# A decoder layer with a mixture of experts: slots given group by group, and the experts' work divided into two bursts and a dense last group

## The chip, the cores and the metric

The kernel runs on one core of one Trainium2 chip. The metric is the device time of one execution in microseconds (us). Before the change the median of 9 runs is 855.45 us, the lowest 849.18, the highest 859.21. The profiled execution took 858.79 us; its span from the first to the last instruction is 857.0 us.

The core has five engines with queues of their own, each working through its instructions in order: PE (TensorE, matrix products), DVE (VectorE), ACT (ScalarE, which also issues DMAs), POOL (GpSimd, which also issues the indirect DMAs) and SP (which here only issues DMAs). They wait for one another by semaphores. SBUF is the on-chip memory of 128 partitions, PSUM holds PE's results, and DRAM holds inputs, outputs and scratch.

## The reference

x and enc are (32, 128, 128): 32 batch rows of 128 tokens with 128 features. One decoder layer in f32, with 16 heads of 8 features:

```
x  = layernorm(x + attn(x, x, x, causal))           # self-attention
x  = layernorm(x + attn(x, enc, enc))               # cross-attention
w  = softmax(x @ router_w + router_b)               # 8 experts
top2 values of w -> softmax -> combine weights of the token's two experts
h  = gelu(x @ e_w1[e] + e_b1[e])                     # 128 -> 512
eo = h @ e_w2[e] + e_b2[e]                           # 512 -> 128
x  = layernorm(x + sum over the token's two experts of combine * eo)
```

The reference computes every expert for every token and weights six of the eight by zero.

## The kernel before

Tokens are handled in groups of G = 4 batch rows; there are 8 groups of self-attention (s0 to s7) and 8 of cross-attention (c0 to c7).

**Attention.** A unit is one batch row of one kind, and there are 64. The list `order` (L607) sets their order: 11 units of s, then c and s in turn, then the 11 units of c that are left, so that LEAD = 11 rows of self-attention run ahead. Each unit takes two half slots (L690 to L705). In half slot h = 2t + half, `both_scores` computes half the heads' scores of unit t, whose row maxima DVE takes (L389), and half the transposed scores of unit t-2, with the maxima subtracted by a matrix product (L366), whose exponentials ACT takes (L397). For s units POOL then zeroes what the causal mask excludes (L401). `split` on POOL cuts the maxima into three bf16 parts, `maxima` turns them, `values` multiplies by V (L431), and `outputs` turns and divides by the sums.

**Work of a group.** A dictionary `table` names what else is traced after which half slot (L634 to L663): fetching the rows, turning them, keys, queries, values, then `project` with the residual and the normalization, `hand_over` from s to c, `keep_x2`, and `route` in five steps. `normalize` (L237) takes mean and variance on DVE and the root on POOL; the last scaling, four instructions (L249), is on the engine passed in: POOL in the attention, DVE at the end. Since tracing order is each engine's order, a step in `table` queues behind what stands before it on that engine.

**Slots.** Each token goes to two experts. The tokens are put into slots, 128 to a block, and a block belongs to one expert. PHASES = ((0, 24), (24, 8)) makes two phases, of 24 and 8 batch rows. `place(p)` (L534) runs once a phase, after its last group was routed: counts by expert, blocks wanted beyond the first of each expert, their starts, every token's rank, and a table of which block has which expert. The first 8 blocks of a phase are fixed, one to an expert; ND more are given as needed, 47 and 15, so the phases have NBL = 55 and 23 blocks. Then `scatter` (L583) sends each batch row twice by indirect DMA on POOL to its slots in DRAM (`xs`), 64 in all, each after a small memset.

**Experts.** After all attention, a loop goes through the 78 blocks (L826). All experts' weights are packed in SBUF (`wpk`: w1, w2, b1, b2 of an expert side by side, 4624 bytes a partition). A fixed block reads its expert's weights in place; for a given block SP loads the expert's number from the table, and a DMA copies the weights from `wpk` to one of five buffers `wd` (L743), four blocks ahead. Rows come four blocks at a time (`fetch_rows`, three buffers), PE turns them, `first_layer` runs 4 matrix products and 4 Gelu on ACT, `second_layer` runs 4 more and DVE adds b2 (L782). Finished blocks go to DRAM (`eo`).

**Gathering.** When a phase's blocks are done, `gather` (L791) fetches each token's two results by indirect DMA on POOL, 64 in all, and `combine` (L802) weights them, adds x2, normalizes and writes out. x2 of all tokens stays in SBUF.

**Loads.** All weights and constants are issued from ACT's queue (L157 to L196), and so is the clearing of `xs` with zeros (L232), 3520 and 1472 KB; the first x is fetched from SP.

Of the kernel before, what the change touches and what calls it, by code (L numbers as in the profile page):

```python
# [17 lines left out]
P = 128  # L18
# [6 lines left out]
PHASES = ((0, 24), (24, 8))  # L25
NP = len(PHASES)
NS = E

ND = [(2 * n * 128 - E) // 128 for _, n in PHASES]
NBL = [NS + n for n in ND]  # L30
XB = 4
W2 = FF
B1 = W2 + FF
B2 = B1 + NFC
WP = B2 + P
VC = 32
RG = 4
NPART = 3
LEAD = 11
EPS = 1e-05  # L40
# [14 lines left out]
def kernel(  # L55
# [39 lines left out]
    keep = ctx.enter_context(tc.tile_pool(name="keep", bufs=1))  # L95
# [4 lines left out]
    ident16 = const.tile([P, P], BF16, name="ident16")  # L100
    nc.vector.tensor_copy(ident16, ident)

# [13 lines left out]

    hm4 = const.tile([P, RG, 4], F32, name="hm4")
# [10 lines left out]
    nc.vector.tensor_reduce(hmask, hm4.rearrange("p g r -> p r g"), AX.X, ALU.add)  # L128


    mp4 = const.tile([P, RG, NPART, 4], F32, name="mp4")
# [5 lines left out]
    mpart = const.tile([P, 4], F32, name="mpart")  # L137
# [9 lines left out]

    apart = const.tile([1, 1], F32, name="apart")
    mhalf = const.tile([P, G], F32, name="mhalf")
    nc.gpsimd.memset(mhalf, -0.5)  # L150
    iota_i = const.tile([P, E], mybir.dt.int32, name="iota_i")
    nc.gpsimd.iota(iota_i, pattern=[[1, E]], base=0, channel_multiplier=0)
    iota_e = const.tile([P, E], F32, name="iota_e")
    nc.vector.tensor_copy(iota_e, iota_i)


    def load(src, shape, name):  # L157
        t = const.tile(shape, F32, name=name)
        nc.scalar.dma_start(out=t, in_=src)
        return t  # L160

    def column(src, name):
        return load(src.rearrange("(p o) -> p o", o=1), [P, 1], name)

    def row(src, n, name):
        return load(src.rearrange("(o n) -> o n", o=1).broadcast_to([P, n]), [P, n], name)

    class Attn:
        def __init__(self, wq, bq, wk, bk, wv, bv, wo, bo, n):
            self.wk = load(wk, [P, P], f"wk{n}")  # L170
            self.bk = column(bk, f"bk{n}")
            self.wq = load(wq, [P, P], f"wq{n}")
            self.bq = column(bq, f"bq{n}")
            self.wv = load(wv, [P, P], f"wv{n}")
            self.bv = column(bv, f"bv{n}")
            self.wo = load(wo, [P, P], f"wo{n}")
            self.bo = row(bo, P, f"bo{n}")

            self.bqm = const.tile([P, 4], F32, name=f"bqm{n}")
            nc.vector.tensor_scalar(self.bqm, hmask, self.bq, None, ALU.mult)  # L180

    sa = Attn(sa_wq, sa_bq, sa_wk, sa_bk, sa_wv, sa_bv, sa_wo, sa_bo, "s")
    ca = Attn(ca_wq, ca_bq, ca_wk, ca_bk, ca_wv, ca_bv, ca_wo, ca_bo, "c")
# [6 lines left out]
    b1 = load(e_b1.rearrange("e (c f) -> (e c) f", f=P), [E * NFC, P], "b1")  # L190


    wpk = const.tile([P, E, WP], F32, name="wpk")
    nc.scalar.dma_start(
        out=wpk[:, :, B2:], in_=e_b2.unsqueeze(0).broadcast_to([P, E, P])
    )  # L196


    def counted(shape, pattern, base, name):
        i = const.tile(shape, I32, name=f"{name}_i")  # L200
        nc.gpsimd.iota(i, pattern=pattern, base=base, channel_multiplier=0)
        f = const.tile(shape, F32, name=name)
        nc.vector.tensor_copy(f, i)
        return f

# [3 lines left out]
        fill=0.0, base=0, channel_multiplier=-1,  # L209
    )  # L210
    NF = max(n for _, n in PHASES) - 1
    full = counted([P, E, NF], [[0, E], [P, NF]], P, "full")
    e_col = counted([P, E, E], [[1, E], [0, E]], 0, "e_col")
    e_row = counted([P, E, E], [[0, E], [1, E]], 0, "e_row")
    lower = const.tile([P, E, E], F32, name="lower")
# [682 lines left out]
```

## Time and profile before

| What | us |
|---|---|
| Profiled execution, its own time | 858.79 |
| Its span, first to last instruction | 857.0 |
| Median of 9 runs | 855.45 |
| Busy in the span: PE | 579.5 |
| PE's weight loads, beside PE | 484.0 |
| DVE | 361.2 |
| ACT | 354.6 |
| POOL | 393.0 |

The mean clock granted to TensorE was 0.867 of full speed. DMA queues moved 73.87 MB, 86 GB/s in the mean.

A busy time is a share of the whole span, and the stages have different limits: read it by stretch. In the chain of work that ended last, "another core or an unknown queue" stands for a wait on something that the profile doesn't name as an instruction; here there is one core. Idle time of an engine costs nothing where another sets the pace.

### The profile page before, as it was taken

The numbers are of one execution on the slowest core, as the hardware profiler recorded it, in microseconds if no ns is written. First come the engines' busy times: TensorE is split into PE (matmuls) and PEld (weight loads), VectorE is DVE, ScalarE is ACT, GpSimd is POOL, SyncE is SP. The second block draws the span as 40 slices with busy tenths as digits, with TensorE's granted clock in tenths as the row PEclk, the third lists the DMA queues.
The fourth block names the chain that finished last, engine by engine and source line by source line (L and its number), as shares of the span: only waits on it lengthen the run. The fifth ranks groups of instructions, "written<-read, shape, count | busy, mean of one in ns | idle before, by whom it ended". The sixth has DMA issues, their size and how long they took to land.

```text
span 857.0 us, 21066 instructions
## 1 busy us (share of the span) xinstructions
PE 579.5 (68%) x8767; PEld 484.0 (56%) x8819; DVE 361.2 (42%) x996; ACT 354.6 (41%) x666; POOL 393.0 (46%) x698
## 2 busy tenths in 40 slices
PE   1488988889989899899989820009999980645200
PEld 0256666667667676677768610009999980645200
DVE  3035555556656566565667540002222210353426
ACT  0225656565666656665665300005555540223100
POOL 5025566536656366563544588870000027155271
PEclk9969999999999999999999755558999995778655
DMA  6800202002010000000000011124999945255121
GB/s 143 244 1 3 76 8 69 16 2 64 15 39 15 2 15 2 14 3 15 3 2 3 9 36 52 52 71 168 335 355 370 342 139 174 91 172 180 51 59 37
DMA packets 66911, 73.87 MB, mean 86 GB/s; under 512 B 6368, under 2 KB 55808, under 8 KB 66816
## 3 DMA queue, kind: packets, MB, share of 16 engines
q1 hardware_dynamic: 43360, 55.32, 18.6%
q10 hardware_dynamic: 19360, 8.81, 3.8%
q0 software_dynamic: 4096, 8.40, 3.3%
q8 instruction: 69, 1.13, 0.6%
q14 instruction: 26, 0.21, 0.1%
HBM read 19.30 MB, written 16.52 MB: 42 GB/s over the span
## 4 chain that ended last, share of the span: by engine, by line
PE 46%; another core or an unknown queue 11%; POOL 11%; DVE 10%; ACT 8%; DMA 5%; issue 5%; SPq 2%; ACTq 2%; POOLq 0%; DVEq 0%
PE po L778 7%; PE ph L761 6%; PE st_c L374 4%; PE st_s L374 4%; PE po_s L431 4%; DMA wd<-wpk 3%; ACT qb_c L327 3%; POOL pr_s L401 2%; PE po_c L431 2%; ACT qb_s L327 2%; POOL gt L797 2%; PE st_c L366 2%; POOL y_c L249 2%; PE st_s L366 2%
## 5 line engine op out<-in xcount | busy, mean ns | idle before, releaser
L797 POOL DMA_INDIRECT gt<-eo,slots x64 | 63.0, 984 | 151.3 <-ACT h L766 124.4
L389 DVE TENSOR_REDUCE m_s<-sc_s 128x8 f32<-128x1024 f32 x64 | 78.2, 1222 | 123.0 <-PE st_s L374 90.2
L401 POOL TENSOR_SCALAR_AFFINE_SELECT pr_s<-pr_s 128x1024 f32<-128x1024 f32 x64 | 69.9, 1096 | 90.2 <-ACT pr_s L397 90.2
L389 DVE TENSOR_REDUCE m_c<-sc_c 128x8 f32<-128x1024 f32 x64 | 78.1, 1220 | 68.4 <-PE st_c L374 48.8
L766 ACT ACTIVATE h<-ph,wd 128x128 f32<-128x128 f32 x248 | 70.6, 370 | 87.3 <-issue 26.8
L397 ACT ACTIVATE pr_s<-st_s 128x1024 f32<-128x1024 f32 x64 | 65.7, 1026 | 74.4 <-PE st_s L374 74.4
L778 PE MATMUL po<-wd,h 128*128 128x128 f32 x496 | 70.7, 289 | 25.4 <-ACT h L766 21.1
L397 ACT ACTIVATE pr_c<-st_c 128x1024 f32<-128x1024 f32 x64 | 65.6, 1025 | 52.6 <-PE st_c L374 51.9
L778 PEld LDWEIGHTS po<-wd,h 128*128 128x128 f32 x496 | 64.8, 204 | 26.5 <-ACT h L766 23.3
L381 PE MATMUL sc_s<-k_s,qb_s 32*128 32x128 f32 x1024 | 78.2, 293 | 0.5 <-issue 0.4
L381 PE MATMUL sc_c<-k_c,qb_c 32*128 32x128 f32 x1024 | 74.9, 284 | 0.6 <-DVE m_c L389 0.3
L761 PE MATMUL ph<-xT,wd 128*128 128x128 f32 x496 | 69.6, 285 | 4.4 <-DMA wd<-wpk 4.4
L589 POOL DMA_INDIRECT xs<-x,slots x64 | 61.8, 966 | 22.8 <-issue 13.7
L374 PE MATMUL st_c<-qb_c,k_c 32*128 32x128 f32 x1024 | 71.9, 278 | 0.0
L374 PEld LDWEIGHTS st_c<-qb_c,k_c 32*128 32x128 f32 x1024 | 70.9, 193 | 0.5
L374 PEld LDWEIGHTS st_s<-qb_s,k_s 32*128 32x128 f32 x1024 | 68.6, 190 | 0.0
L374 PE MATMUL st_s<-qb_s,k_s 32*128 32x128 f32 x1024 | 68.3, 272 | 0.0
L381 PEld LDWEIGHTS sc_s<-k_s,qb_s 32*128 32x128 f32 x1024 | 65.4, 194 | 3.2 <-issue 2.5
L761 PEld LDWEIGHTS ph<-xT,wd 128*128 128x128 f32 x496 | 63.5, 200 | 6.2 <-DMA wd<-wpk 6.0
L381 PEld LDWEIGHTS sc_c<-k_c,qb_c 32*128 32x128 f32 x1024 | 62.6, 187 | 1.8 <-DVE m_c L389 1.8
L782 DVE TENSOR_TENSOR ot<-po,wd 128x128 f32<-128x128 f32 x62 | 18.0, 291 | 103.8 <-PE po L778 97.3
L751 PE MATMUL px<-ident,xt 128*128 128x128 f32 x78 | 12.7, 288 | 70.8 <-DMA xg<-in_x_dram 70.8
(203 smaller groups left out, 1173.1 us busy)
## 6 DMA issues: line engine op xcount, KB each, us to landing
wd<-wpk SPq DMA_DIRECT2D x62, 578.0 KB
xt<-xs SPq DMA_DIRECT2D x18, 256.0 KB
eo<-ot SPq DMA_DIRECT2D x18, 256.0 KB
wpk<-in_L_xattn_e_w_dram SPq DMA_DIRECT2D x16, 256.0 KB
xs<-zero ACTq DMA_DIRECT2D x1, 3520.0 KB
xg<-in_x_dram SPq DMA_DIRECT2D x8, 256.0 KB
eg<-in_ctx_dram SPq DMA_DIRECT2D x8, 256.0 KB
out_dram<-acc ACTq DMA_DIRECT2D x8, 256.0 KB
```

Source lines behind the costliest of these rows:

```text
L327: nc.scalar.activation(gr.qb[:, :, r, :], pq, AF.Identity, bias=gr.w.bqm[:, r : r + 1], scale=hmask[:, r : r + 1],)
L374: nc.tensor.matmul(st[:, i, r, :], lhsT=old.group.k[rowsof(g), old.b, :], rhs=old.group.qb[rowsof(g), old.b, r, :], start=False, stop=r == 3,)
L381: nc.tensor.matmul(sc[:, i, r, :], lhsT=new.group.qb[rowsof(g), new.b, r, :], rhs=new.group.k[rowsof(g), new.b, :], start=not new.masked, ...
L389: nc.vector.tensor_reduce(new.m[:, 8 * half : 8 * half + 8], sc.rearrange("p i r k -> p (i r) k"), AX.X, ALU.max,)
L397: nc.scalar.activation(old.pr[:, hs, :], st.rearrange("p i r k -> p (i r) k"), AF.Exp, scale=SCALE)
L401: nc.gpsimd.affine_select(out=old.pr[:, hs, :], in_=old.pr[:, hs, :], pattern=[[0, 8], [1, P]], compare_op=ALU.is_ge, fill=0.0, base=0, ch ...
L431: nc.tensor.matmul(po[VC * r : VC * r + VC, g, :], lhsT=u.group.v[:, u.b, 4 * g + r, :], rhs=u.pr[:, 4 * g + r, :], start=True, stop=True,)
L589: i = nc.gpsimd.indirect_dma_start(out=xs[p][:, :], out_offset=bass.IndirectOffsetOnAxis(ap=slots[:, k, b : b + 1], axis=0), in_=x2[:, b, ...
L761: nc.tensor.matmul(ph[:, c, :], lhsT=w[:, c * P : (c + 1) * P], rhs=xTs[g][:, j, :], start=True, stop=True,)
L766: nc.scalar.activation(hs[i][:, c, :], ph[:, c, :], AF.Gelu, bias=w[:, B1 + c : B1 + c + 1])
L778: nc.tensor.matmul(pos[g][:, j, :], lhsT=h[:, c, :], rhs=w[:, W2 + c * P : W2 + (c + 1) * P], start=c == 0, stop=c == NFC - 1,)
L797: nc.gpsimd.indirect_dma_start(out=gts[gi][:, k, b, :], out_offset=None, in_=eo[p][:, :], in_offset=bass.IndirectOffsetOnAxis(ap=slots[:, ...
```

## The change

- **Phases.** PHASES is now given in groups, ((0, 4), (4, 3)): groups 0 to 3 (16 batch rows, 39 blocks) and 4 to 6 (12 batch rows, 31 blocks). Group 7 (LAST) takes no slots.
- **Slots by group.** `place` runs for each group, in five steps behind its `route`. It keeps by phase how full each expert's open block is, where that block stands, the next free block, and sums for the table. The group's scatters follow, one batch row to a half slot.
- **First burst.** All 39 blocks of phase 0 run in one stretch before half slot 117 (2 * BURST + 3) with no attention between; weights and rows are prefetched from half slot 114. Its gathers follow from half slot 118, one batch row (two indirect DMAs) to a half slot, with the combining in six steps.
- **Second burst.** When the attention is done and the last rows of phase 1 are scattered, its 31 blocks run.
- **Dense group.** Group 7 then runs on all 8 experts, 512 tokens at a time; every expert's result is weighted by `comb`, which is zero where the expert wasn't chosen, and added to x2. The gathers and the combining of phase 1 are traced beside it, three half slots to an expert.
- **Weights** are packed in DRAM; every block and every dense expert loads them into one of the five buffers. x2 goes to DRAM as well and is read back by `combine`; only the dense group keeps it in SBUF.
- **Normalization.** The scaling is always on DVE and in a step of its own.
- **Loads.** The first x is issued first of all, on SP; the rows that are broadcast to all partitions go to SP, matrices and columns stay on ACT, `xs` is cleared from SP at half slots 38 and 40.
- **V** is stored with heads 9 elements apart (before 32); the 32 columns that PE loads for a head run into the next heads, and those rows of the result are not used.
- PSUM: a block's hidden layer uses the attention's score banks, two in turn (before three of its own); hidden tiles have two buffers (before three), fetched rows one (before three).

```diff
-PHASES = ((0, 24), (24, 8))
+PHASES = ((0, 4), (4, 3))
+LAST = 7
-ND = [(2 * n * 128 - E) // 128 for _, n in PHASES]
+ND = [(2 * n * G * 128 - E) // 128 for _, n in PHASES]
+AHEAD = 4
+VS = HD + 1
+BURST = 57
...
+    fetch(groups["s", 0])
...
+    def row(src, n, name, queue=nc.sync):
...
-    for p in range(NP):
-        nc.scalar.dma_start(out=xs[p].rearrange("(n p) d -> p n d", p=P), in_=bc(zero, 1, NBL[p]))
...
-    wpk = const.tile([P, E, WP], F32, name="wpk")
+    wpk = tc.dram_tile([E, P, WP], F32, name="wpk")
+    x2d = tc.dram_tile([B, P, P], F32, name="x2d")
...
         nc.gpsimd.tensor_tensor(rs, rs, mhalf, ALU.pow)
+        yield
         for t in range(G):
-            engine.tensor_scalar(
+            nc.vector.tensor_scalar(
                 y[:, t, :], y[:, t, :], mv[:, t, 0:1], rs[:, t : t + 1], ALU.subtract, ALU.mult
             )
...
+    def place(gr, ph):
...
+        nc.vector.tensor_tensor(tot, ph.fill, pn, ALU.add)
...
+        nc.vector.tensor_reduce(start, first, AX.X, ALU.add)
+        yield
...
+        nc.vector.tensor_tensor(pos, pr, bc(ph.fill, 1, G), ALU.add)
+        yield
...
+        nc.vector.tensor_copy(slots[:, :, bs], sf)
+        yield
...
+        nc.vector.tensor_copy(ph.free, end[:, E - 1 : E])
+        yield
...
+    def pack(e):
+        nc.sync.dma_start(out=wpk[e, :, :W2], in_=e_w1[e])
...
+    def clear(p):
+        nc.sync.dma_start(out=xs[p].rearrange("(n p) d -> p n d", p=P), in_=bc(zero, 1, NBL[p]))
...
+    class Blocks:
...
+        def prepare(self):
+            for i in range(AHEAD):
+                self.fetch_weights(i)
+            self.fetch_rows(0)
+
+        def run(self, beside):
+
+            self.turn(0)
+            for i in range(self.n):
+                self.fetch_weights(i + AHEAD)
+                self.first_layer(i)
+                self.second_layer(i - 1)
+                if i % XB == min(2, self.width(i // XB) - 1):
+                    self.turn(i // XB + 1)
+                beside()
+            self.second_layer(self.n - 1)
...
+    class Dense:
...
+        def first_layer(self, e):
...
+                for c in (2 * i, 2 * i + 1):
+                    nc.tensor.matmul(
+                        hid[:, c % 2], lhsT=w[:, c * P : (c + 1) * P], rhs=self.gr.x2T,
+                        start=True, stop=True,
+                    )
+                    nc.scalar.activation(
+                        self.h[e][:, c], hid[:, c % 2], AF.Gelu, bias=w[:, B1 + c : B1 + c + 1]
+                    )
+
+        def second_layer(self, e):
...
+            for b in range(G):
+                for c in range(NFC):
+                    nc.tensor.matmul(
+                        po[:, b, :], lhsT=h[:, c, b, :], rhs=w[:, W2 + c * P : W2 + (c + 1) * P],
+                        start=c == 0, stop=c == NFC - 1,
+                    )
+            for b in range(G):
+                share = self.comb[:, b, e : e + 1]
+                for term in (w[:, B2:], po[:, b, :]):
+                    nc.vector.scalar_tensor_tensor(
+                        acc[:, b, :], term, share, acc[:, b, :], ALU.mult, ALU.add
+                    )
...
+        for ph in phases:
+            g0, n = PHASES[ph.p]
+            if g0 <= gi < g0 + n:
+                h = steps(h, 5, lambda c=c, ph=ph: place(c, ph))
+                for b in range(G):
+                    h = at(h, scatter, c, ph, b)
+    for e in range(E):
+        at(4 + 4 * e, pack, e)
+    at(3, pack_biases)
+    for p in range(NP):
+        at(38 + 2 * p, clear, p)
+
+    bursts = [Blocks(ph) for ph in phases]
+    dense = Dense(groups["c", LAST])
+    at(2 * BURST, bursts[0].prepare)
+    h = 2 * BURST + 4
+    for gi in range(PHASES[0][0], PHASES[0][0] + PHASES[0][1]):
+        for b in range(G):
+            h = at(h, gather, groups["c", gi], b)
+        steps(h + 1, 6, lambda c=groups["c", gi]: combine(c))
...
+        for h in range(-2, 2 * BURST + 3):
+            half_slot(h)
+        bursts[0].run(lambda: None)
+        h = 2 * BURST + 3
+        while h < 2 * (len(units) + 3) or any(f is scatter for c in table.values() for f, *_ in c):
+            half_slot(h)
+            h += 1
+        bursts[1].prepare()
...
+        bursts[1].run(beside)
...
+        for e in range(3):
+            dense.fetch(e)
+        dense.share()
...
+        dense.first_layer(0)
         for e in range(E):
+            dense.fetch(e + 3)
+            dense.first_layer(e + 1)
+            dense.second_layer(e)
+            for _ in range(3):
+                beside()
+        for _ in finish(dense.gr):
+            pass
```

## The prediction

> **What bounds the kernel now.** I read the stretches first: busy time per engine in stretches cut where the work changes. Columns: stretch, its length, then PE, PEld, DVE, ACT, POOL busy us with instruction counts, granted clock, DMA share, GB/s.
>
> ```profile
> 214.00:321.00 107.00, 95.62 (x1840) 75.34 (x1856) 64.54 (x166) 65.93 (x88) 60.11 (x115) 1.00 0.06 17
> ...
> 488.00:508.00 20.00, 6.86 (x44) 4.82 (x42) 8.29 (x63) 1.89 (x5) 16.99 (x29) 0.59 0.11 37
> 508.00:579.00 71.00, 0.39 (x2) 0.42 (x3) 5.04 (x14) 0.00 (x0) 57.04 (x107) 0.50 0.17 56
> 579.00:708.00 129.00, 122.61 (x1039) 119.86 (x1037) 27.83 (x74) 69.79 (x241) 5.52 (x6) 0.97 0.80 284
> 708.00:733.00 25.00, 0.03 (x1) 0.07 (x1) 0.58 (x2) 1.14 (x4) 17.21 (x19) 0.54 0.49 166
> 733.00:807.00 74.00, 41.74 (x287) 40.42 (x287) 32.30 (x111) 19.11 (x68) 29.37 (x32) 0.80 0.38 130
> 807.00:857.00 50.00, 0.00 (x0) 0.00 (x0) 24.06 (x88) 0.00 (x0) 21.10 (x24) 0.50 0.18 51
> ```
>
> PE binds where it works (107 us of attention, 95.6 busy; 129 us of experts, 122.6 busy, the DMA nearly full as well), and it stands still while POOL sends rows (71 us), fetches them (25 us) and in the tail (50 us). Next the costliest groups, for the two indirect DMAs:
>
> ```profile
> L797 POOL DMA_INDIRECT gt<-eo,slots x64 | 63.0, 984 | 151.3 <-ACT h L766 124.4
> L589 POOL DMA_INDIRECT xs<-x,slots x64 | 61.8, 966 | 22.8 <-issue 13.7
> ```
>
> In order of time one scatter follows another after 1.26 us, one gather after 1.25 us: 64 of each are 80 us of POOL. Last the chain that ended last, in order of time (start, us, what):
>
> ```profile
> 19.57 11.36 ACTq L232
> 30.96 1.28 ACT L311
> ...
> 195.16 1.06 POOL rs_c L247
> 196.31 3.14 POOL y_c L249 x4
> 199.45 2.12 POOL pr_s L401 x2
> 201.61 1.08 PE po_s L431 x32
> ...
> 507.80 70.14 another core or an unknown queue
> ...
> 708.20 24.30 another core or an unknown queue
> ```
>
> ACT can copy nothing until it has issued the clearing of the slots at 30.9; in the attention a normalization on POOL holds back the mask of the probabilities and so PE; then the chain waits for rows on their way. So three things bind: POOL's indirect DMAs, PE's experts, and the start.
>
> **The change part by part.** The sum goes by this execution: span 857.0, 858.8 with what lies around it, 3.3 over the median of 855.45. A half slot is one step of the attention's order; the last exponential of each lets me count them: half slot 0 starts at 38.0, half slot 117 at 438.
>
> *Start.* ACT's 32 DMA issues end at 30.9, the two clearings alone taking 11.94. After, ACT issues 19 before its first copy. The first 16 took until 10.7, 0.62 each with their stalls: 12. From ACT's table load to the first scores lie 7.0 (30.96 to 37.98), so scores start at 19.5, 18.5 sooner. The rows go to SP behind x (ten issues of 0.45, done by about 6; the copies they feed come later than ACT's). The clearings cost SP their 12 us at half slots 38 and 40; the next fetch behind them is at 50, ten half slots (33 us) on: nothing. Without that room it would cost the 12.
>
> *Attention up to half slot 117* (400 us before). Off POOL: 4 scalings of 0.8 us in each of 13 groups, 41 us, of which the chain holds about 17 (y_c, 2% of the span). DVE gets them at 0.28 each, 1.1 a group, in 64.5 of 107 busy. On to POOL: scatters of four groups, 32 x 1.26 = 40 us, in two to each half slot of 3.35 us, beside masks of 1.1 each; all fits POOL's room (60.1 of 107 busy) or nothing does: 0 to 40. Placing is now done per group: some 22 small DVE instructions of 0.2 to 0.3 in five steps, 5 us a group, 20 in all, queued ahead of the maxima, for which PE waits: 0 to 20. I take 8 gained, 12 lost in scatters (a mask waits for what stands before it, as in the rows of 195 to 201), 8 lost in placing: +12; ends -20 and +55. Shorter memsets and tighter values change nothing after the start (same loads, same copies). Writing x2 out and packing weights on SP is covered by the idle DMA (share 0.06); uncovered it would be some 20 transfers of about 1 us.
>
> *First burst.* 16 rows of tokens give 39 blocks. Between 598.3 and 693.6 the experts' first activations came every 2.07 us, for 592 KB of weights (578 KB on the page) and 131 KB of rows. PE alone does 1.90 (three of 1.79 and one of 2.22 with its transposes). The weights now come from DRAM, not SBUF. Bounds from DMA packets of this trace: 4624 bytes SBUF to SBUF 179 ns, 2048 bytes from DRAM 84 ns, mostly 101 in the mean: 390 to 320 GB/s over 16 engines, 1.85 to 2.26 us a block. I take 2.07: 39 x 2.07 = 81, two table loads of 1.28, 2 of fill: 86. The prefetch stays five buffers deep; the rows have one buffer instead of three, and four blocks (8 us) for a transfer of 1 to 2 us.
> By the Trainium skill, "DMA: Bandwidth & Descriptors", section "Where 436 GB/s comes from", transfers between HBM and SBUF end at about 358 GB/s while copies within SBUF may reach 435, which speaks against taking the weights out of SBUF. By it a block's 723 KB take 2.02 us, an estimate; with that the sum would be 4 less, since the row before is not faster.
>
> *From the first burst to the second.* PE has 44 us of attention left (438 to 482), but POOL must do in order: 32 gathers (40), 24 scatters (30), 6 splits of maxima (6.6), three groups' x2 at 2.6 (7.8), seven normalizations' powers at 1.3 (9.4): 94. Before it 2.9 for the last block's landing (write issued 698.0, gather 701.0), behind it 4.0 from the last scatter to the first layer (576.5 to 580.5): 101. So the scatter stall isn't gone, it is late next in another place: before, this stretch and the scatters took 141 (438 to 579). Ends 80 (only the indirect DMAs) and 142 (POOL and attention one after the other).
> The Trainium skill, "SBUF — State Buffer", section "Who interferes with whom", says a DVE tensor_scalar in its two-port mode and GpSimd exclude each other for a whole instruction. In the trace four scalings beside a gather took 1.33 instead of 1.11, two gathers 1.15 and 1.27 instead of 0.94. By these rows the move of the scalings costs 0.8 a group; by the rule up to four gathers' length, 3.8 a group, some 15 in this stretch, and the sum would be 779.
>
> *Second burst.* 31 x 2.07 + 1.3 = 65.5, with nothing beside it; before, 23 blocks cost 25 stalled and 74 us beside gathers.
>
> *Last group on all experts.* 8 experts, each 4 matmuls 128x512 (1.14 each, from pq_c) and 16 of 128x128 (0.89 for four): 8.1; 65 in all, 32 tiles of work in place of some 8 plus padding. Weights are fetched behind the last block's write: 4. DVE: 8 additions of 0.35 an expert plus three groups' combining of 6.7: 43 of 65. 24 gathers, 30 of POOL, lie beside it; uncovered they cost 30. A fetch beside gathers took 3.6 to 4.5 (four in 14.4 and in 18.0), under 8.1. Together 69.
>
> *Tail.* Additions 3, normalization 5.5 (from the last group's rows: 847.8 to 853.7), landing 3.4: 12, for 50 before.
>
> Sum: 19.5 + 412 + 86 + 101 + 65.5 + 69 + 12 = 765 of span; 91.8 less than 857.0, so **764** against the median.
>
> **The rivals.**
> *A, attention choked.* Scatters and placing fall wholly on the path: +55 in place of +12, and 5 more in the burst's wait: 812. For it: the mask waits on POOL already in the chain. Against: POOL and DVE are 60% busy there.
> *B, engines crawl beside gathers.* From 708 to 733 PE, ACT and DVE did almost nothing while 24 gathers ran back to back. If that comes with every long run of gathers, attention can't overlap (+41) nor the dense experts (+30): 835. Against: beside eight gathers (750 to 760) DVE worked on.
> *C, the weights starve PE: slower than before.* In both bursts each block waits for its weights from DRAM. The nearest slow row is four fetches in 14.42: 3.6 us a block, 70 x 1.53 = +107: 871. It decides from 3.37 us a block (2.07 + 91/70). Against: that row was beside gathers, and no gather is beside a burst; packets from DRAM are as quick as others.
> *D, better.* Scalings gain their 17, the rest hides, blocks run at PE's 1.90: 764 - 29 - 12 = 723.
>
> **How the numbers follow.** Forecast 0.60, its own range 738 to 795; A 0.14, B 0.12, C 0.07, D 0.07. The range of 722 to 833 leaves out C and some of A, B and D. All but C end more than 0.5% (4.3 us, about what this measurement can tell from no change) below 855: faster 0.91, same 0.02, slower 0.07.
>
> **What would show it.** First scores near 19.5; a stretch of about 86 us near 430 with PE at 9 tenths; then about 100 us with POOL near full and PE half idle; two expert stretches of 65 with no gap over 5; no PE-free tail over 15. Wrong would be: activations in a burst more than 2.3 us apart (C), half slots of 4 us and more around the scatters (A), PE idle exactly as long as the gathers run (B).

## The result, and the profile after

The changed kernel takes 824.93 us (median of 19 runs, 818.57 to 832.63) where the kernel before takes 855.50 (62 runs): a ratio of 0.9642, 95% interval 0.9624 to 0.966. It is faster, as forecast, and 825 lies inside the range of 722 to 833; but 31 us are gained where 91 were forecast. The profiled execution took 828.16, its span is 826.4, against 765 in the sum: 61 are missing.

The stretches of the changed kernel, cut where the work changes (stretch, length, then PE, PEld, DVE, ACT, POOL busy us with counts, granted clock, DMA share, GB/s):

```profile
45.00:448.00 403.00, 346.87 (x6427) 270.27 (x6481) 258.94 (x672) 227.11 (x302) 205.45 (x415) 0.98 0.18 49
448.00:534.00 86.00, 81.59 (x740) 77.89 (x732) 21.57 (x56) 52.01 (x165) 2.70 (x5) 1.00 0.85 296
534.00:661.00 127.00, 64.20 (x812) 52.33 (x806) 73.62 (x307) 26.38 (x36) 81.11 (x124) 0.64 0.24 73
661.00:729.00 68.00, 63.86 (x523) 61.59 (x523) 14.23 (x42) 35.46 (x124) 0.00 (x0) 0.96 0.85 289
729.00:812.00 83.00, 65.10 (x320) 40.70 (x320) 34.59 (x125) 22.00 (x32) 27.06 (x30) 0.92 0.31 95
812.00:827.00 15.00, 0.00 (x0) 0.00 (x0) 5.36 (x20) 0.00 (x0) 1.27 (x2) 0.63 0.12 34
```

The two bursts (86 and 68 us) are as forecast, PE busy 95% in the one and 94% in the other. The stretch between them, 127, has no engine above 65%: PE 64, DVE 74, POOL 81. Nothing that is busy binds there; things wait for one another. And in the dense part PE is busy 65 of 83.

The costliest groups, for the indirect DMAs; their durations are nearly as before (992 ns for 984, 1018 for 966), so a single DMA has hardly become slower:

```profile
L786 POOL DMA_INDIRECT gt<-eo,slots x56 | 55.6, 992 | 95.5 <-DMA eo<-ot 79.9
...
L640 POOL DMA_INDIRECT xs<-x,slots x56 | 57.0, 1018 | 10.9 <-issue 10.4
```

The chain that ended last, at its start (start, us, what):

```profile
1.26 4.03 DMA bks<-in_L_xattn_sa_bk_dram
...
5.30 4.57 DMA wos<-in_L_xattn_sa_wo_dram
...
9.89 4.07 DMA wqc<-in_L_xattn_ca_wq_dram
...
13.99 2.30 DMA lngT<-in_L_xattn_ln_g_dram
...
16.29 1.28 ACT L314
```

ACT reaches its table load at 16.3, not at the 12 that I had summed, because between its issues it waits for transfers to land.

Term by term, on the boundaries of the sum (the last column is the same kernel on another chip, of which more below):

| Term | forecast | recorded profile | another chip |
|---|---|---|---|
| start and attention, to the first burst | 431.5 | 448 | 432 |
| first burst | 86 | 86 | 88 |
| between the bursts | 101 | 127 | 117 |
| second burst | 65.5 | 68 | 64 |
| dense, to PE's end | 69 | 83 | 83.5 |
| tail | 12 | 15 | 15 |
| span | 765 | 826.4 | 799.3 |

### The profile page after: what moved, and what is told of

The parts are those of the page before. It is cut to its first block, busy times and chain, and to the rows that moved or that the text cites. A ratio compares the mean times of both kernels' runs of the same rounds, so it can differ in the third digit from the quotient of the medians.

```text
span 826.4 us, 21600 instructions
## 1 busy us (share of the span) xinstructions
PE 645.7 (78%) x8943; PEld 518.1 (63%) x8995; DVE 416.8 (50%) x1242; ACT 370.2 (45%) x668; POOL 327.2 (40%) x616
## 4 chain that ended last, share of the span: by engine, by line
PE 55%; DVE 14%; DMA 10%; ACT 7%; another core or an unknown queue 4%; issue 4%; POOL 4%; SPq 0%; POOLq 0%; ACTq 0%; DVEq 0%
DMA wd<-wpk 7%; PE st_s L375 5%; PE ph L733 5%; PE phd L848 4%; PE po L751 4%; PE st_c L375 4%; PE pod L861 3%; DVE m_c L390 3%; PE po_s L434 3%; PE po_c L434 3%; DVE m_s L390 3%; PE sc_c L382 3%; PE st_s L367 2%; PE sc_s L362 2%
## 5 line engine op out<-in xcount | busy, mean ns | idle before, releaser
L738 ACT ACTIVATE h<-ph,wd 128x128 f32<-128x128 f32 x280 | 80.0, 369 | 71.1 <-PE ph L733 40.0
L398 ACT ACTIVATE pr_s<-st_s 128x1024 f32<-128x1024 f32 x64 | 65.7, 1026 | 89.4 <-PE st_s L375 69.3
L786 POOL DMA_INDIRECT gt<-eo,slots x56 | 55.6, 992 | 95.5 <-DMA eo<-ot 79.9
L382 PE MATMUL sc_c<-k_c,qb_c 32*128 32x128 f32 x1024 | 81.2, 293 | 3.9 <-issue 1.6
L733 PE MATMUL ph<-xT,wd 128*128 128x128 f32 x560 | 78.4, 285 | 5.9 <-DMA wd<-wpk 2.8
L375 PE MATMUL st_c<-qb_c,k_c 32*128 32x128 f32 x1024 | 77.8, 287 | 0.5 <-issue 0.5
L375 PEld LDWEIGHTS st_c<-qb_c,k_c 32*128 32x128 f32 x1024 | 75.5, 201 | 1.5 <-issue 0.8
L733 PEld LDWEIGHTS ph<-xT,wd 128*128 128x128 f32 x560 | 69.4, 195 | 10.8 <-DMA wd<-wpk 6.0
L382 PEld LDWEIGHTS sc_c<-k_c,qb_c 32*128 32x128 f32 x1024 | 66.9, 193 | 7.2 <-DVE m_c L390 3.2
L416 POOL CAST m<-m_c 128x16 bf16<-128x16 f32 x32 | 6.4, 198 | 151.5 <-DVE m_c L390 151.5
L640 POOL DMA_INDIRECT xs<-x,slots x56 | 57.0, 1018 | 10.9 <-issue 10.4
```

The lines of the kernel that those rows point to most:

```text
L375: nc.tensor.matmul(st[:, i, r, :], lhsT=old.group.k[rowsof(g), old.b, :], rhs=old.group.qb[rowsof(g), old.b, r, :], start=False, stop=r == 3,)
L382: nc.tensor.matmul(sc[:, i, r, :], lhsT=new.group.qb[rowsof(g), new.b, r, :], rhs=new.group.k[rowsof(g), new.b, :], start=not new.masked, ...
L398: nc.scalar.activation(old.pr[:, hs, :], st.rearrange("p i r k -> p (i r) k"), AF.Exp, scale=SCALE)
L640: i = nc.gpsimd.indirect_dma_start(out=xs[ph.p][:, :], out_offset=bass.IndirectOffsetOnAxis(ap=slots[:, k, t : t + 1], axis=0), in_=gr.x2[ ...
L733: nc.tensor.matmul(hid[:, c, :], lhsT=w[:, c * P : (c + 1) * P], rhs=self.xT[i // XB][:, i % XB, :], start=True, stop=True,)
L738: nc.scalar.activation(self.h[i][:, c, :], hid[:, c, :], AF.Gelu, bias=w[:, B1 + c : B1 + c + 1])
```

## The experiments

Two suspects came out of the traces. **T**: PE stands still while POOL issues an indirect DMA. In the recorded profile four scatters ran from 288.1 to 293.0, and products of PE that had been issued at 290.4 signalled their end at 293.9, while ACT and DVE worked at their usual pace; from issue to signal, products far from an indirect DMA mostly take 0.24 to 0.6, those beside one 1.6 in the median and up to 9.8. **Q**: PE merely waits for masks and maxima that stand behind the DMAs on POOL's queue. T2 is T with a stall that lasts until a whole run of DMAs is over. Times are compared within kernels whose kernel before took the same.

### 1. The suspects by themselves

A kernel of stages; in each, PE works through twelve groups of eight products while one suspect runs:

```diff
+g = stage("alone", g, tensor, nothing)
+g = stage("sends", g, tensor, lambda g: sends(g, 12))
+g = stage("masks", g, tensor, lambda g: mask(g, 12))
+g = stage("apart", g, tensor, lambda g: sends(g, 6, fill=1))
+...
```

> Not the layer: a kernel of stages one behind the other, in each of which PE (or ACT, or DVE) works through the same chain, 96 matrix products of 128x128 in f32 in twelve groups, alone or beside one suspect: 12 scatters back to back, 12 gathers, 12 masks of POOL without any DMA, 6 scatters with a mask between them, 12 plain DMAs from SP, 12 scatters of 32 rows, 12 plain DMAs from POOL; then bf16 products, ACT copies and DVE products, each alone and beside 12 scatters. No chain reads what the suspects write. Theory T (PE stands still while POOL issues an indirect DMA, about 0.8 us for each, from 24.8 us lost over 32 scatters in the attention): the chain is 8 to 12 us longer beside 12 scatters or 12 gathers, 4 to 6 longer with 6 scatters apart, unchanged beside masks and beside SP's DMAs; ACT and DVE unchanged. Rival T2 (PE is held until a whole run of indirect DMAs is over): beside 12 scatters the chain ends some 15 us late, with masks between them less than 2. Rival Q (PE merely waited for masks and maxima that stood behind the DMAs on POOL): every chain of PE takes the same time within 1 us.

> The stages once more. On a chip where the kernel before takes 832: every chain of PE again 21.7 us of products beside whatever it has. On one where it takes 855: if the stall belongs to that chip, the chain of 96 products ends some 8 to 15 us later beside 12 scatters or 12 gathers, and not beside masks or SP's DMAs; with masks between the scatters it tells whether a run's length matters. If it ends in 21.7 there as well, the stall needs something that the layer does and the stages don't.

> The stages of the first two runs of them again. Where the kernel before takes 832: 96 products in 21.7 us beside whatever stands beside them, as on the two chips before. Where it takes 855: beside 12 scatters or 12 gathers the chain ends 8 to 15 us later if the stall of the first chip shows in plain products; not beside masks, nor beside SP's DMAs.

The first two runs were on chips where the kernel before takes 832, the third on one where it takes 858.5, like the recorded one. Length of each chain, from the end of the stage ahead to its own last copy:

| Chain, beside | before takes 832 (both runs) | before takes 858 |
|---|---|---|
| f32, nothing | 22.08 | 22.08 |
| f32, 12 scatters | 22.08 | 31.25 |
| f32, 12 gathers | 22.08 | 30.17 |
| f32, 12 scatters of 32 rows | 22.08 | 33.18 |
| f32, 6 scatters with a mask behind each | 22.08 | 22.08 |
| f32, 12 masks; 12 plain DMAs from SP; 12 from POOL | 22.08 | 22.08 |
| bf16, nothing | 6.22 | 6.22 |
| bf16, 12 scatters | 6.22 | 19.08 |
| ACT, alone and with 12 scatters | 8.12 and 8.12 | 8.13 and 8.13 |
| DVE, alone and with 12 scatters | 8.98 and 8.98 | 8.97 and 8.98 |

The costliest groups of PE in the third run (busy, mean ns, idle before):

```profile
L102 PE MATMUL mm_sends<-g_alone,ident 128*128 128x128 f32 x192 | 26.8, 301 | 4.5 <-issue 4.0 <-ACT g_alone L107 0.4
...
L102 PE MATMUL mm_alone<-g_warm,ident 128*128 128x128 f32 x192 | 21.7, 276 | 0.4 <-ACT g_warm L107 0.4
...
L102 PE MATMUL mm_apart<-g_masks,ident 128*128 128x128 f32 x192 | 21.7, 276 | 0.4 <-ACT g_masks L107 0.4
```

and the same group in the second run:

```profile
L102 PE MATMUL mm_sends<-g_alone,ident 128*128 128x128 f32 x192 | 21.7, 276 | 0.4 <-ACT g_alone L107 0.4
```

So the stall is real, PE's alone, needs nothing of the layer, and shows on some chips and not on others. (Each chip was seen in one session only, so chip and session aren't told apart.) Back to back, 0.3 us apart, 12 DMAs cost 8 to 13; 6 scatters with a mask of 1.1 us behind each cost nothing. That is neither T, which gave 4 to 6 for those, nor T2, which gave 15 for a run of twelve. The 6 are also half as many, so the stages alone don't tell the gap from the number; experiment 10 has gaps in the layer. Smaller DMAs, which follow one another sooner, cost more. What in the chip does it stays open.

### 2. The changed kernel on both kinds of chip

> The changed kernel itself, unchanged, on whichever chip the runs beside it get. On the chip of the four runs before, the kernel before the change took 832 where it took 855 on the first, and no product of PE ended late beside an indirect DMA, in the layer with one DMA to a half slot (173 products beside one: 0.24 to 1.08 us from issue to end, far from one the same) or in the stages. If the stall beside indirect DMAs belongs to the first chip: half slots 59 to 61 take 3.3 to 3.7 each here as before the change, plus what masks and maxima wait for on POOL, some 3 to 5 a group (from the run with fillers: 390.5 from half slot 4 to 116), so 390 to 395 in place of 402.8, and the time is 800 to 806. If the stall comes with pairs of DMAs on any chip, 402 and the same ratio of 0.964.

> The changed kernel again. Where the kernel before takes 832: half slot 4 to 116 in 389 to 391, the stretch between the bursts 120 to 122, span 799. Where it takes 855: 402 to 404, 127 to 131 and 826, with products of PE that end 2 to 10 us late beside indirect DMAs.

On the first kind 799.08 against 831.77 before, a ratio of 0.9589 (0.9553 to 0.9625); on the other 828.75 against 858.51, one run of each. Lengths of half slots 59 to 63, from one exponential to the next, and of all from 4 to 116 (the last two rows are the next two experiments):

```
                           59    60    61    62    63    4 to 116
changed, recorded          6.06  6.15  5.25  2.45  2.93  402.8
changed, 828.75            6.78  5.50  5.24  2.46  2.92  403.8
changed, 799.08            3.67  3.25  3.32  4.92  4.93  389.6
fillers for scatters       3.67  3.25  3.32  5.86  4.41  390.5
one scatter to a half slot 3.68  3.25  3.32  2.72  2.92  375.6
```

Where PE isn't stalled the attention takes 13.5 more than before (376.1), close to the 12 of the sum; the stall adds 13 there, and the stretch between the bursts is 10 longer with it. Dense and tail are the same on both. Stretches on the first kind:

```profile
520.00:637.00 117.00, 52.00 (x811) 44.04 (x809) 75.33 (x307) 25.77 (x36) 80.71 (x124) 0.70 0.27 81
637.00:701.00 64.00, 61.00 (x515) 59.02 (x515) 13.42 (x37) 35.41 (x124) 0.00 (x0) 0.98 0.88 303
701.00:787.00 86.00, 65.74 (x326) 41.11 (x324) 37.33 (x137) 22.04 (x33) 27.04 (x30) 0.92 0.30 95
```

34 of the 61 missing are here too, where no product ends late beside a DMA (0.24 to 1.08). They need another cause.

### 3. The kernel before, beside it

> The kernel before the change, to have its profile on the chip of the runs beside it. If its 855 on the first chip against 832 here is the stall beside indirect DMAs: the blocks that stood between 701 and 735 beside 24 gathers take 2.1 each here, no product of PE ends late, and the attention is the same (376.1 from half slot 4 to 116).

832.06; half slot 4 to 116 in 376.0, and no product ends late. But the blocks don't run through: activations stop from 711 to 730 here as well.

```profile
704.00:730.00 26.00, 10.14 (x91) 9.95 (x90) 8.89 (x29) 4.56 (x16) 19.89 (x23) 0.78 0.54 187
730.00:781.00 51.00, 28.73 (x183) 28.00 (x183) 23.80 (x83) 13.35 (x48) 25.57 (x28) 0.77 0.47 159
```

By the chain that is an ordinary queue. A root of a normalization stands behind the 24 gathers on POOL until 725.3, DVE waits for it, and a block's addition of b2 stands behind that on DVE:

```profile
725.68 1.05 POOL rs_m L247
726.76 1.34 DVE acc L249 x4
...
729.46 0.29 DVE ot L782
```

In the recorded profile the 25 us from 708 to 733 are not this queue. There the addition of b2 comes 1.8 us after the end of the last of the 24 gathers (730.7), and the combining with its root only behind it:

```profile
732.53 0.30 DVE ot L782
...
744.93 0.35 DVE acc L809
...
749.09 1.05 POOL rs_m L247
```

Between 708.1 and 732.5 PE's products signalled an end only six times, 3.6 to 5.9 us apart, and ACT and DVE, which wait for them, did four Gelu and this one addition: the stall of experiment 1. PE got less far beside the gathers, so more is left behind them: 287 products and 74 us (733 to 807), here 183 and 51. These 23 are most of the 26.7 between the two spans (857.0 and 830.3). Since the kernel before loses that much on such a chip too, the ratio is nearly the same on both kinds.

### 4. Fillers in place of the scatters

```diff
-            i = nc.gpsimd.indirect_dma_start(out=xs[ph.p][:, :], ...)
+            if ph.p == 0:
+                nc.gpsimd.affine_select(out=idle, in_=idle, ...)
+                continue
```

> Left out: the 32 scatters of the first phase; each is replaced by a POOL instruction of about the same length (0.95 us) that moves nothing, so the first burst works on zeros. Last exponential of half slot 4 to that of 116 took 402.8 with the scatters and 376.1 before the change. T (the DMA itself stops PE): 377 to 382, and the time falls to about 801. Q (masks and maxima wait on POOL behind whatever stands there): about 402, time about 825.

390.5 (row above), where the scatters themselves give 389.6 on such a chip, and 798.84 in all, where they give 799.08: the fillers saved nothing, which is Q. A mask waits for what stands before it on POOL, whatever it is. That 798.84 is near T's number is the chip's doing.

### 5. One indirect DMA to a half slot

```diff
-                for b in range(G):
-                    h = at(h, scatter, c, ph, b)
+                for b in range(G):
+                    for k in range(2):
+                        h = at(h, scatter, c, ph, b, (k,))
```

> One indirect DMA to a half slot in place of two, for scatters and gathers alike; as many of them in all. T: the cost goes with their number, so half slot 4 to 116 stays near 402 and the time within 3 us of 825. Q: with 1.25 us of DMA and 1.1 of mask in a half slot of 3.35 POOL is no longer the bound: half slot 4 to 116 falls to about 382, time about 800. T2: runs of one are over after 1 us: about 388, time about 805. Between the bursts the gathers take twice as many half slots, which can hold back the last scatters: up to 10 longer there.

375.6: the 14 are gone and T falls on this kind of chip. Yet the time is 807.27 (0.9714, 0.9675 to 0.9754), 8 above the 799 of the changed kernel on a like chip. Beside the dense experts the gathers, now in twice as many steps, end at 782.4, behind the experts' last activation (766.9), and from there to the end it takes 38 in place of 22: 16 lost there, and 4 in the second burst.

### 6. No indirect DMA at all

```diff
-            nc.gpsimd.indirect_dma_start(out=gr.gt[:, k, b, :], ...)
+            nc.sync.dma_start(out=gr.gt[:, k, b, :], in_=eo[p][P * t : P * t + P, :])
```

> Left out: the placing of rows; every one of the 56 scatters and 56 gathers is a plain DMA of the same 64 KB from SP to or from fixed rows, so POOL issues none. T and Q both expect the attention without its 27 us (half slot 4 to 116 in 376). Between the bursts T expects PE's 44 us of attention and the last group's routing and placing behind them, 80 to 90 in place of 127; dense 70 to 75 in place of 83. Time 745 to 765. If less than 30 us are gained, indirect DMAs are not where the gain went.

760.11, and attention in 372.6. Between the bursts it still takes 101, not 80 to 90, from the first activation of the one's last block to the first of the other (121 with the DMAs; so measured below as well). POOL, which the prediction had made the bound, is busy for 22 in that stretch:

```profile
503.00:601.00 98.00, 50.77 (x823) 42.66 (x815) 74.14 (x307) 26.21 (x36) 22.24 (x44) 0.73 0.33 97
```

The chain there is DVE's, line after line the combining of the first phase:

```profile
545.24 3.14 DVE acc L791 x4
...
549.39 1.05 DVE acc L791 x4
...
554.40 1.04 DVE acc L282 x4
555.46 0.69 DVE acc L800
...
558.54 1.05 DVE acc L791 x4
```

The routing and placing of the second phase's last group, for which the second burst waits, stands behind these on DVE. The dense part, for which T had 70 to 75, is as long as with the DMAs: 69.3 from its first activation to the end of its last.

### 7. The combining moved beside the second burst

```diff
-        steps(h + 1, 6, lambda c=groups["c", gi]: combine(c))
+        steps(LATE + 6 * gi, 6, lambda c=groups["c", gi]: combine(c))
```

> The combining of the first phase's four groups (about 7 us of DVE each) moves from between the bursts to beside the second burst, with four buffers for gathered rows in place of two. Theory D (between the bursts DVE, not POOL, is the bound: in the run without indirect DMAs the same stretch still took 101 us, and its chain was DVE's instructions, the combining first): the stretch from the last activation of the first burst to the first of the second gets 20 to 28 us shorter, the second burst stays at 66 to 69, the time falls by 20 to 28 against the unchanged kernel beside it. The prediction's own view (POOL's 94 us of work is the bound there): within 3 us of the unchanged kernel.

From last to first activation 108.5 for 120.9, but the second burst 79.5 for 63.1, and in all 804.01 (0.9658, 0.961 to 0.9706), 5 more than the changed kernel. By the trace eight gathers and six scatters run one behind the other on POOL from 581.8 to 599.4, ahead of the last group's scatters; and in the burst the chain waits for x2, fetched only when its turn comes, with a block's addition behind it on DVE:

```profile
652.59 6.97 DMA acc<-x2d
...
660.71 0.15 DVE ot L756
```

So neither DVE nor POOL alone is the bound. With x2 fetched before the burst, groups written out from POOL's queue, and the gathers of groups 2 and 3 behind the last scatters:

```diff
+        if gi == 2:
+            h = END
+        at(END - 4 + gi, fetch_x2, groups["c", gi])
-        nc.sync.dma_start(out=out[...], in_=gr.acc)
+        nc.gpsimd.dma_start(out=out[...], in_=gr.acc)
```

> As in the run that moved the combining, but SP has nothing left to wait for beside the second burst: x2 is fetched before that burst into four buffers, and the finished groups are written out from POOL's queue; and the gathers of groups 2 and 3 (16 of the 32) go behind the last scatters. In the run that only moved the combining, the stretch between the bursts got 12.4 shorter (121 to 108.5, on the second chip) and the second burst 16.4 longer. Theory D' (both are true: DVE's combining and POOL's gathers hold the last slots back; and beside the burst it was SP's queue, where weights stood behind an output waiting for DVE): the stretch between the bursts 90 to 100, second burst 63 to 67, time 20 to 28 below the changed kernel. If DVE's work itself slows the burst: second burst near 78, little gained.

772.69 (0.9294, 0.9259 to 0.9329), 26 below the changed kernel; 94 between the activations and 64.5 for the burst:

```profile
519.00:609.00 90.00, 49.69 (x811) 42.10 (x810) 53.62 (x219) 25.91 (x36) 63.40 (x106) 0.77 0.27 84
609.00:676.00 67.00, 63.15 (x519) 60.52 (x518) 33.75 (x123) 35.37 (x124) 17.20 (x22) 0.97 0.90 314
```

DVE's 20 us have moved from the first line to the second, where PE covers them. These edits were made together, so the share of each isn't known, nor what sets the 94 that are left.

### 8. The start

```diff
-            self.wo = load(wo, [P, P], f"wo{n}")
+            self.wo = load(wo, [P, P], f"wo{n}", nc.sync)
-    ca = Attn(ca_wq, ..., ca_wo, "c")
+    ca = Attn(ca_wq, ..., "c", nc.sync)
```

> Only the five loads of self-attention that the first scores need are issued on ACT; the other 23 go behind x on SP, and the products of biases come after half slot 0. Theory L (ACT's first copy waits because the loads of both queues share eight semaphores in turn, each free only when its last transfer has landed): the first copy falls from 17.6 to 7 or 8 and the first exponential from 45 to 34 to 37; all that follows is as much earlier. Rival (the first scores wait on POOL's setting up of constants): the first exponential stays within 2 of 45.

First copy at 5.4, first exponential at 32.7 for 42.3 in the changed kernel on such a chip, time 792.69 (one run) for 799.08: 6.4 of the 9.6 by which the first exponential is earlier. The rival, which had it within 2 of 45, is out. The chain's start:

```profile
0.79 2.90 DMA wks<-in_L_xattn_sa_wk_dram
...
4.08 1.22 ACT L318
...
5.38 0.59 ACT kvT_s L318
```

Both queues take turns on the same eight semaphores (numbers 100 to 107 in the trace); a ninth DMA waits until the first has landed, on whichever queue it stands. Two queues share that limit: ACT was done at 16.3 with 19 of the 29 loads, where before the loads from one queue had taken 19.0 (30.9 less 11.9 for the clearings).

### 9. The dense experts

In the changed kernel the chain has two waits for an activation in each expert (kernel of experiment 2, first kind of chip):

```profile
735.14 0.88 PE phd L848 x2
736.09 0.70 ACT hd L852
736.83 2.00 PE phd L848 x4
738.85 0.70 ACT hd L852
739.59 1.12 PE phd L848 x2
740.72 3.57 PE pod L861 x32
```

The second product into a PSUM tile waits until the activation has read the first, which lies in its other half.

```diff
                 for c in (2 * i, 2 * i + 1):
                     nc.tensor.matmul(hid[:, c % 2], ...)
+                for c in (2 * i, 2 * i + 1):
                     nc.scalar.activation(self.h[e][:, c], hid[:, c % 2], ...)
...
             if i >= self.n:
+                if self is bursts[1]:
+                    dense.fetch(i - self.n)
                 return
```

> Two edits in the dense part alone: both products into one PSUM tile are issued before the two activations that read it, and the experts' first weights are fetched while the last blocks of the second burst run. Theory P (by the chain, PE waits twice in every expert for an activation of 0.70 although it writes the other half of the tile, 9.14 an expert in place of PE's 7.57; and 4.1 for the first weights): 7.6 an expert, 12 us, and 4 more, so 14 to 17 us below the changed kernel. Rival (the gathers on POOL beside it, or DVE's eight additions an expert, set the 9.14): at most the 4.

773.51 (0.9286, 0.9253 to 0.9319), 25.6 below, more than the 14 to 17 expected. Without the waits an expert takes 7.02, less than PE's 7.57 that I had read off (of eight experts 17 us), and the first dense activation comes 2.7 behind the last block's, for 8.0:

```profile
705.97 3.57 PE pod L864 x32
709.54 3.44 PE phd L850 x8
712.98 3.57 PE pod L864 x32
```

### 10. All of it

```diff
+ the start of 8, one scatter of the first phase to a half slot,
+ the stretch between the bursts as at the end of 7, dense as in 9
```

> All of it: the five urgent loads alone on ACT (9.6 of start by the run before), one scatter of the first phase to a half slot (14 of the 389.6 from half slot 4 to 116 on the second chip), the stretch between the bursts as in the run that frees SP (20 to 28), dense as in the run of two edits (14 to 17). If they add, 58 to 68 below the changed kernel: about 735 where that takes 799 and the kernel before 832, a ratio of 0.88.

> The better version again. Where the kernel before takes 832: 725 to 730. Where it takes 855: scatters one to a half slot leave the attention at 380 to 388 if single DMAs stall PE little, the stretch between the bursts 95 to 105, and 24 indirect DMAs beside the second burst cost it up to 25 (as 24 gathers beside experts did in the kernel before): 735 to 765.

727.12 against 832.66: 0.8752 (0.8714 to 0.879), faster than both kernels, 72 below the changed one on a like chip (799.08). From that to this version the spans differ by 75: start 11, half slots 4 to 116 11, between the bursts 26, from the last block's activation to the end 28.

```profile
495.00:590.00 95.00, 55.22 (x865) 47.09 (x864) 54.72 (x221) 28.66 (x41) 63.77 (x107) 0.77 0.26 82
590.00:654.00 64.00, 61.86 (x511) 59.35 (x510) 32.61 (x118) 35.03 (x124) 16.84 (x21) 0.97 0.97 338
654.00:712.00 58.00, 56.94 (x328) 41.44 (x327) 35.79 (x130) 20.56 (x34) 27.76 (x31) 1.00 0.40 128
```

On a chip that stalls it takes 774.61 (before 858.51): above the 735 to 765 expected, as the dense part, with 16 gathers in a row, loses some 10 that I had not counted. The half slots 4 to 116 (388) end at the top of what was expected, too, and the stretch between the bursts (106) just above it. The 388.1 for 378.8 on the other kind show that single scatters cost PE something too: beside those that lie at least 2.3 us from the next, a product signals its end 0.74 us after its issue in the median and 3.56 at most, for 0.30 and 0.61 on the other kind. Putting a mask behind each of the 40 gathers beside burst and dense experts:

```diff
+            if gr.gi >= 2:
+                nc.gpsimd.affine_select(out=idle, in_=idle, ...)
```

> The better version with a mask of POOL over an unused tile (1.1 us) behind each of the 40 gathers that lie beside the second burst and the dense experts. In the stages on the chip that stalls, 12 scatters back to back cost PE's chain 9.2 us and 6 with a mask behind each cost nothing. On such a chip (before 855 to 859): second burst from 77.5 to 64 to 67 from its first activation to its last, dense from 57.4 to 47 to 50, time 752 to 760 in place of 774.6. On the others (before 832): POOL is idle there, so 725 to 731 as without the masks. If on a stalling chip little is gained, gaps alone don't free PE.

773.66 against 854.5 (0.9064, 0.9039 to 0.909): nothing gained. The gaps do free PE for the most part: on the two stalling chips the second burst from first to last activation is 68.2 with them and 77.5 without (63.7 where nothing stalls), the dense activations 47.8 and 57.4 (47.8 where nothing stalls). But the last gathers end at 740 as without them, now behind PE's end at 734, and the combining that lay beside PE comes after it:

```profile
677.00:736.00 59.00, 57.42 (x333) 41.91 (x331) 50.00 (x73) 21.04 (x36) 48.89 (x48) 1.00 0.39 118
736.00:771.00 35.00, 0.00 (x0) 0.00 (x0) 25.92 (x83) 0.00 (x0) 8.40 (x11) 0.53 0.10 28
```

A shorter gap, or gaps for the burst alone, wasn't tried.

## Why the prediction was right in its sign and wrong in its size

- *"From the first burst to the second"*, 101, is the step that failed most: 127, of which 10 are the stall and 16 are there without it. I summed POOL's instructions and took the sum for the time. Two things were left out. The combining of the first phase's four groups is DVE's work in this stretch (I had counted combining on DVE for the dense part alone), and the last group's routing and placing stands behind it. And POOL doesn't work through: 81 busy of 127. Taking POOL's DMAs away left 101; taking the combining away left 108; easing both gave 94. In the recorded profile the upper end of 142 (POOL and attention one after the other) was nearer than the value I took; on a chip without the stall, at 117, it was not.
- *"Last group on all experts"*, 69: 83. The term was PE's work, 8.1 an expert. The chain has 9.14, because of an order of instructions that stands in the code: product, activation, product into one tile. With the order changed it is 7.02, so the price of PE's work was if anything high. The rest is the wait for the first weights with the two first layers behind it, where I had taken 4.
- *"Attention up to half slot 117"*, +12: 26.7 by the half slots 4 to 116 in the recorded profile, 13.5 on a chip without the stall. The sum held there; of its terms the scatters measured 17 for 12 (372.6 without them), scalings and placing together a gain of 3.5 for nothing. The other 13 are the stall, which this term had not.
- *"Start"*, 18.5: 13.2 by the first exponential (58.2 to 45.0). I priced ACT's issues by what 16 of them had taken; with a second queue issuing at the same time, the shared semaphores were the limit.
- *First burst, second burst*: right. C (weights starve PE) is excluded: 38 steps of a block from 455.7 to 531.3 are 1.99 each, at 296 GB/s. By the Trainium skill, "DMA: Bandwidth & Descriptors", section "Where 436 GB/s comes from", a block is 2.02, an estimate. The trace's 1.99 is nearer to it than to my 2.07. Whether the transfers set the 1.99 isn't shown, as PE is busy 95% there.
- *B, engines crawl beside gathers*, had 835, the price nearest to the time, for reasons that hold only in part. Its row, the 25 us of the kernel before, is such a crawl on a chip that stalls, but PE's alone: ACT and DVE wait for its products (experiment 3). Its two terms did not come: of the 41 between the bursts 10 did, and dense, where B put 30, loses nothing to it in the changed kernel (83 and 83.5). What came was 13 beside scatters, where B had nothing. 34 of the 61 missing have nothing to do with it.
- *A*'s 55 for scatters and placing was too much: 13.5, or 27 with the stall. Its sign did come, half slots of 4 us and more around the scatters (up to 5.1, with the stall 6.9), but it was no good sign: half slots of 4.7 stand in the kernel before as well. *D* wasn't reached by the changed kernel; 727 took four more edits.
- *Scalings on DVE*: the Trainium skill, "SBUF — State Buffer", section "Who interferes with whom", gave, by an estimate, up to 15 more between the bursts. In the changed kernel's recorded trace 41 of the 96 scalings overlap an indirect DMA: 0.36 us in the mean and 0.57 at most, for 0.34 alone. So the 15 didn't come. Seven that began under one of POOL's masks (1.1) ended with it, after 0.73 to 1.12, some 4 us in all, which is as that rule has it. The section also says that PE never waits on anyone there; on two chips of five it waited, 9.2 us for 12 scatters.
- *The sums*: 857.0 less 765 is 92.0 and not 91.8, which moves nothing. The attention's terms give ends of -17 (as D has it) and, with the 8 gained, +52, where I wrote -20 and +55.

## What to carry to other kernels

Where several engines share a stretch and none is near full, the longest queue is a lower end and not the time: write down what the stretch's last consumer waits for, and on each engine what stands in front of it, work carried over from the stage before included. Work that no later stage needs soon (here, combining finished groups) goes behind that chain, beside a stage bound by another engine, with its inputs fetched ahead. And an engine's busy time is its price only if the order of instructions lets it run through: look for two writes into one tile with a read between them.

## What the runs showed of the hardware

- On two of the five chips of these runs, and in the recorded profiles, PE nearly stands still while POOL issues indirect DMAs back to back: 12 scatters lengthen a chain of f32 products from 22.08 to 31.25, one of bf16 from 6.22 to 19.08. A gap takes most of it away: 6 scatters with a mask of 1.1 us behind each cost that chain nothing, but in the layer the second burst beside gathers so spaced is 68.2 (77.5 without gaps, 63.7 without the stall), and half slots 4 to 116 with single scatters, mostly 2.4 to 4.9 us apart, take 388.1 for 378.8. On the other three chips the same kernels show none of it. Cause open, and chip and session not told apart.
- The kernel before takes 832 on some chips and 855 on others; half slots 4 to 116, without an indirect DMA, take 376.0 and 376.1, and 23 of the 26.7 between two profiled runs come of what PE left undone beside 24 gathers.
- The DMAs of ACT and SP wait for one another's landings through eight semaphores used in turn: in the changed kernel ACT's issues wait until 5.3 and 9.9 for the loads of bks and wos. With 5 of its 19 loads left on ACT, its first copy came at 5.4 in place of 17.6 in the recorded profile; fewer issues and shorter waits aren't separated there.
- A scaling on DVE (0.34 us) that starts under a mask on POOL ends with the mask, after up to 1.12; beside an indirect DMA it took 0.57 at most.
